# The feed-forward's first product as seven block products, its GELU moved behind the next copy, and sums moved to GpSimd and ScalarE

## The chip, the core and the metric

The kernel runs on one core of one Trainium2 chip. The time is device microseconds of one launch, from start to end. It was measured in three runs; their median is 1070.18 us, the lowest 1069.54 us, the highest 1071.64 us.

## What is computed

The input is a matrix of 4096 rows (tokens) of 256 numbers, all float32. Each row is normalised; the result feeds two branches, and the output is the input plus both.

```python
xn = layernorm(x)
# branch 1: attention in windows of 64 rows, then a feed-forward
x1 = xn + attention(xn) @ Wo + bo
x2 = layernorm(x1) * gamma + beta
h  = gelu(x2 @ W1 + b1)            # W1: 256 x 1024
branch1 = x2 + h @ W2 + b2         # W2: 1024 x 256
# branch 2: two of 8 experts for each token, weighted by their shares
branch2 = sum over the two of share * (silu(gate(xn) * up(xn)) @ down + bias)
out = x + branch1 + branch2
```

The change touches the last stage only: `h`, the second product, and the sum of everything.

## The kernel before, in words

Tokens are sorted by expert. A long first part of the kernel computes, in each step, attention for four of the eight heads of 256 tokens and one expert unit side by side; the experts' results are written to `done`, a table in device memory with one row for each (token, expert) pair. Some further units run under a condition. The last of them ends at 847 us on TensorE. From there on only the feed-forward is left.

The feed-forward works on eight groups of 512 tokens, `g = 0..7` (L1547 to L1576). The order of every engine's instructions is that of the code: nothing is rearranged, and each engine takes its instructions strictly one after another. In one turn of the loop, for group `g`:

- SyncE loads the rows of group `g + 2` (`second_loads`, L1186): `x2` (two buffers) and the input rows into the sum `acc` (four buffers).
- `hidden(g)` (L1222): the first product. The hidden units are eight blocks of 128; for each, two matmuls (one for each half of the 256 input features) of 128 x 512 run into one PSUM bank, and ScalarE takes the bank with bias and GELU into `hT`. There are seven banks for everything in this stage, used in turn.
- `second_base(g + 1)` (L1202): on VectorE, `acc += beta + b2`, `scaled = x2 * gamma`, `acc += scaled`, each over 1024 numbers a partition.
- `combined(g - 1)` (L1281): on VectorE, eight instructions add the rows of the two experts, times their shares, to `acc`.
- `turned2(g + 1)` (L1209): TensorE transposes `x2`, and ScalarE writes it with `gamma` and `beta` as `x2T`, the input of `hidden(g + 1)`.
- `second_norm(g + 2)` (L1190): ScalarE normalises the loaded rows.
- `picked(g)` (L1266): GpSimd issues eight gathers from `done`, one for 128 tokens and one of their two experts.
- `second(g - 1)` (L1289), the second product, of the group before: seven block products of 16 matmuls each, in place of eight (p1, p2, p6, p5, p7, p3, p4, in the order of the code), with sums of blocks prepared before and sums of results after. VectorE adds the results to `acc`. `sums_of_hidden(g)` (L1254) prepares this for the group's own second product: four additions of 1024 numbers a partition on VectorE, put between the pieces of `second(g - 1)`.
- SyncE stores `acc` of group `g - 1`.

At `g = 0` there is no second product and no transpose, so `hidden(0)` and `hidden(1)` follow one another on TensorE. The sums of W2's blocks are made once on GpSimd (`sums_of_weights`, L1248). On GpSimd there is nothing else in this stage but the gathers.

Of the kernel before, what the change touches and what calls it, by code (L numbers as in the profile page):

```python
# [32 lines left out]
F32 = mybir.dt.float32  # L33
# [3 lines left out]
ALU = mybir.AluOpType  # L37
# [66 lines left out]
def block_kernel(ctx: ExitStack, tc: tile.TileContext, a: dict, out: bass.AP):  # L104
# [1097 lines left out]
    def second_base(g, acc, x2):  # L1202

        scaled = accp.tile([P, TG, D], F32, tag="scaled", name=f"scaled{g}", bufs=1)
        nc.vector.tensor_tensor(acc, acc, bcast(beta_b2, TG, 1), ALU.add)
        nc.vector.tensor_tensor(scaled, x2, bcast(gamma, TG, 1), ALU.mult)
        nc.vector.tensor_tensor(acc, acc, scaled, ALU.add)

    def turned2(g, x2):  # L1209
        x2T = turns.tile([P, DC, G], F32, tag="x2T", name=f"x2T{g}")  # L1210
        for c in range(DC):
            pt = bank(f"pt2_{g}_{c}")
            for t in range(TG):
                nc.tensor.transpose(  # L1214
                    pt[:, t * P : (t + 1) * P], x2[:, t, c * P : (c + 1) * P], ident
                )
            nc.scalar.activation(
                x2T[:, c, :], pt, AF.Identity, bias=beta_c[:, c : c + 1], scale=gamma_c[:, c : c + 1]
            )
        return x2T  # L1220

    def hidden(g, x2T):  # L1222
        hT = hf.tile([P, FC1, G], F32, tag="hf", name=f"hf{g}")
        for f in range(FC1):
            ph = bank(f"ph{g}_{f}")
            for c in range(DC):
                nc.tensor.matmul(  # L1227
                    ph,
                    W1[:, c, f * P : (f + 1) * P],
                    x2T[:, c, :],  # L1230
                    start=(c == 0),
                    stop=(c == DC - 1),
                )
            nc.scalar.activation(hT[:, f, :], ph, AF.Gelu, bias=b1[:, f : f + 1])  # L1234
        return hT

# [28 lines left out]

    def picked(g):  # L1266

        ys = []
        for i in range(g * TG, (g + 1) * TG):
            for k in range(2):  # L1270
                y = got.tile([P, D], F32, tag="got", name=f"got{i}_{k}")
                nc.gpsimd.indirect_dma_start(  # L1272
                    out=y,
                    out_offset=None,
                    in_=done,
                    in_offset=bass.IndirectOffsetOnAxis(ap=slot[:, k, i : i + 1], axis=0),
                )
                ys.append(y)
        return ys

    def combined(g, acc, ys):  # L1281
        for n, y in enumerate(ys):
            t, k = n // 2, n % 2
            i = g * TG + t
            nc.vector.scalar_tensor_tensor(  # L1285
                acc[:, t, :], y, share[:, k, i : i + 1], acc[:, t, :], ALU.mult, ALU.add
            )

    def second(g, acc, hT, v):  # L1289

        t1, t2 = slice(0, 2), slice(2, 4)
        u = hf.tile([P, 2, P], F32, tag="u", name=f"u{g}")

        def product(n, left, right):
            pb = bank(f"s{g}_{n}").rearrange("p (t n) -> p t n", n=P)[:, 0:2]
            for t in range(2):
                for f in range(FH):
                    nc.tensor.matmul(  # L1298
                        pb[:, t, :],
                        left[:, f, t * P : (t + 1) * P],  # L1300
                        right[:, f, :],
                        start=(f == 0),
                        stop=(f == FH - 1),
                    )
# [12 lines left out]
        p6 = product(6, v[:, 1], V2[:, 1])  # L1317
        nc.vector.tensor_tensor(u, p6, u, ALU.add)
        add(t1, C2, u)
        yield  # L1320
        p5 = product(5, v[:, 0], V2[:, 0])
        add(t1, C2, p5)
        add(t2, C2, p5)
        yield
        p7 = product(7, v[:, 2], V2[:, 2])
        nc.vector.tensor_tensor(u, p7, u, ALU.add)
        add(t2, C1, u)
        add(t2, C2, u)
        yield
        p3 = product(3, v[:, 3], W2[:, F_HI, C2])  # L1330
        add(t1, C2, p3)
        yield
        p4 = product(4, hT[:, F_HI, B:], V2[:, 3])
        add(t2, C1, p4)
        yield
# [35 lines left out]
    for b in range(ALWAYS):  # L1371
# [63 lines left out]
        if b == STEPS:  # L1435
            att.close()
            wf = pool(ctx, "wf", right)
            accp = pool(ctx, "accp", right, bufs=4)
            V2 = wf.tile([P, 4, FC1 // 2, P], F32, tag="V2", name="V2")
            x2s = {n: second_rows(n) for n in range(2)}  # L1440
            W1, W2 = matrix(wf, "W1", F1, DC), matrix(wf, "W2", D, FC1)
            b1 = column("b1", FC1, wf)
            gamma, beta, b2 = (row(n, D, wf) for n in ("gamma", "beta", "b2"))
            gamma_c, beta_c = column("gamma_c", DC, wf), column("beta_c", DC, wf)
            beta_b2 = wf.tile([P, D], F32, tag="beta_b2", name="beta_b2")
            shift2 = wf.tile([P, NT], F32, tag="shift2", name="shift2")
            turns = pool(ctx, "turns", right, bufs=2)

            late = pool(late_done, "late", right)
            other.update({n: late for n in range(ALWAYS, BLOCKS, 3)})  # L1450
            load_unit(ALWAYS)
            for n in range(ALWAYS, BLOCKS):
                xs[n] = gather(n)
            x2s = {n: (second_inputs(n), x2) for n, x2 in x2s.items()}
        if b == STEPS + 1:
            sums_of_weights()
        if b == ALWAYS - 1:
            load_unit(ALWAYS + 1)
        if b + 1 < ALWAYS:
# [52 lines left out]


    x2Ts = {n: turned2(n, x2s[n][1]) for n in range(2)}

    for b in range(ALWAYS, BLOCKS):
        nc.gpsimd.memset(xs[b], 0.0)
# [18 lines left out]
    late_done.close()  # L1536
    experts_done.close()
    hf = pool(ctx, "hf", right, bufs=2)
    got = pool(ctx, "got", right, bufs=8)
    second_base(0, *x2s[0])  # L1540
    last = None

    def some(steps, n):
        for _ in range(n):
            next(steps, None)

    for g in range(NG):  # L1547
        if g + 2 < NG:
            x2s[g + 2] = second_loads(g + 2)
        hT = hidden(g, x2Ts.pop(g))  # L1550
        if g + 1 < NG:
            second_base(g + 1, *x2s[g + 1])
        if g > 0:
            acc = x2s.pop(g - 1)[0]
            combined(g - 1, acc, ys)
        if 0 < g < NG - 1:
            x2Ts[g + 1] = turned2(g + 1, x2s[g + 1][1])
        if g + 2 < NG:
            second_norm(g + 2, x2s[g + 2][1])
        ys = picked(g)  # L1560
        outs = second(g - 1, acc, *last) if g > 0 else iter(())
        some(outs, 2)
        sums = sums_of_hidden(g, hT)
        last = hT, next(sums)
        some(outs, 2)
        some(sums, 1)
        some(outs, 3)
        if g > 0:
            store(g - 1, 0, TG, acc)
    acc = x2s.pop(NG - 1)[0]  # L1570
    combined(NG - 1, acc, ys)
    outs = second(NG - 1, acc, *last)
    some(outs, 6)
    store(NG - 1, 0, 2, acc)
    some(outs, 1)
    store(NG - 1, 2, 2, acc)  # L1576
# [86 lines left out]
```

## Time and profile before

| | |
|---|---|
| median of three runs | 1070.18 us |
| the profiled execution: its own time | 1067.22 us |
| its span in the profile | 1065.5 us |
| DVE (VectorE) busy over the span | 755.9 us, 71% |
| ACT (ScalarE) busy | 572.0 us, 54% |
| POOL (GpSimd) busy | 586.8 us, 55% |
| from 901.3 to 928.5 us, one turn of the loop: PE, DVE, ACT, POOL busy | 27.20, 15.87, 9.05, 7.94 us |
| granted TensorE clock in that turn | 1.00 |

A profile row names an engine, a line of the code, the operation, what it writes and reads, how many instructions it stands for, and how long they took. PE is TensorE, DVE is VectorE, ACT is ScalarE and POOL is GpSimd. A matmul of float32 appears as two records. In a list in order of time, the first number is the start in us from the span's start, the second the duration, and a bracket at the end tells how long the engine had been idle and who released it. In a list of groups, the numbers after the bar are busy us and mean ns of one, then idle us before them with the releaser.

### The profile page before, as it was taken

What the parts mean: (1) busy time and instruction counts of PE and PEld (TensorE: products, weight loads), DVE (VectorE), ACT (ScalarE), POOL (GpSimd) and SP (SyncE); (2) the same over time, 40 slices, a digit from 0 to 9 for tenths busy, and PEclk for the clock granted to TensorE, in tenths of its full rate; (3) what the DMA queues carried; (4) which work ended last, traced back from release to release, by engine and by line L of the source; (5) the groups of instructions that cost most, each with busy time, mean ns of one, the idle gap of its engine ahead of it and who ended that gap; (6) DMA issues with size and microseconds to landing.
All of it is one profiled execution on the core that took longest, in us unless ns stands there. A gap on an engine that the chain in (4) does not pass through costs nothing. (4 is left out here: it accounts for less than half of the span.)

```text
span 1065.5 us, 20424 instructions
## 1 busy us (share of the span) xinstructions
PE 1056.0 (99%) x7278; PEld 859.9 (81%) x7278; DVE 755.9 (71%) x1852; ACT 572.0 (54%) x1329; POOL 586.8 (55%) x706
## 2 busy tenths in 40 slices
PE   9999999999999999999999999999999999999998
PEld 6578887887888888888888888888888757777778
DVE  6667876877787687788888988888542455555546
ACT  4527566656656557756665666566454353333320
POOL 5418765675666666776777777777520053222220
PEclk9999999999999999999999999999999999999999
DMA  8226444435345344534543544445585343333111
GB/s 282 81 91 217 140 158 164 165 139 184 120 155 187 111 156 164 193 139 166 173 168 130 189 163 165 139 173 179 179 272 179 134 136 109 100 99 98 61 60 41
DMA packets 61047, 158.67 MB, mean 149 GB/s; under 512 B 6576, under 2 KB 46896, under 8 KB 56208
## 3 DMA queue, kind: packets, MB, share of 16 engines
q1 hardware_dynamic: 53632, 139.33, 37.7%
q0 software_dynamic: 6480, 17.70, 5.2%
q8 instruction: 59, 0.97, 0.4%
q10 hardware_dynamic: 832, 0.30, 0.1%
q14 instruction: 44, 0.36, 0.1%
HBM read 135.43 MB, written 21.89 MB: 148 GB/s over the span
## 5 line engine op out<-in xcount | busy, mean ns | idle before, releaser
L839 PE MATMUL gu<-xsT,wg 128*128 128x256 f32 (+1 forms) x1632 | 362.8, 369 | 0.0
L839 PEld LDWEIGHTS gu<-xsT,wg 128*128 128x128 f32 x1632 | 288.8, 190 | 46.0 <-DVE nm L1057 9.0
L1272 POOL DMA_INDIRECT got<-done,slot x64 | 64.5, 1008 | 175.8 <-DVE acc L1285 106.9
L847 ACT ACTIVATE gs<-gu,wg 128x256 f32<-128x256 f32 (+1 forms) x204 | 92.0, 452 | 112.8 <-PE gu L839 108.4
L1084 POOL TENSOR_TENSOR pr<-pr 128x256 f32<-128x256 f32 x128 | 113.5, 887 | 64.1 <-ACT pr L1072 64.1
L848 DVE SCALAR_TENSOR_TENSOR hT<-gu,wg,gs 128x256 f32<-128x256 f32 (+1 forms) x204 | 91.9, 462 | 73.8 <-ACT gs L847 73.8
L1085 POOL TENSOR_TENSOR pr<-pr,ident 128x256 f32<-128x256 f32 x128 | 132.8, 1038 | 10.0
L1072 ACT ACTIVATE pr<-pr,nm 128x256 f32<-128x256 f32 x256 | 126.8, 497 | 1.0 <-ACT xsT L831 0.6
L1227 PE MATMUL ph<-x2T,W 128*128 128x512 f32 x256 | 111.0, 592 | 0.0
L1234 ACT ACTIVATE hf<-ph,b 128x512 f32<-128x512 f32 x64 | 43.8, 687 | 122.0 <-PE ph L1227 55.3
L880 ACT ACTIVATE hT<-hT 128x512 f32<-128x512 f32 (+2 forms) x179 | 84.9, 485 | 32.6 <-DVE hT L848 22.4
L1057 DVE CUSTOM_DVE_ANT_0 pr<-ps,mask 128x256 f32<-128x256 f32 x256 | 90.7, 420 | 16.1 <-PE ps L1043 16.1
L814 POOL DMA_INDIRECT xs<-xnd,token x71 | 68.8, 969 | 50.7 <-DVE paired_tiles L781 33.1
L1227 PEld LDWEIGHTS ph<-x2T,W 128*128 128x128 f32 x256 | 48.2, 190 | 57.9 <-issue 54.5
L1102 DVE TENSOR_TENSOR pr<-pr,rec 128x1024 f32<-128x1024 f32 x32 | 39.2, 1225 | 42.5 <-POOL pr L1084 42.5
L1115 POOL TENSOR_TENSOR xd<-xd,same 128x256 f32<-128x256 f32 x32 | 19.7, 615 | 84.2 <-DVE same L1113 84.1
L1308 DVE TENSOR_TENSOR acc<-u,acc 128x256 f32<-128x256 f32 x32 | 12.9, 423 | 68.4 <-ACT u L1311 67.9
L929 POOL TENSOR_TENSOR ts<-wd 128x384 f32<-128x384 f32 x54 | 54.0, 1000 | 2.1
L1072 ACT ACT_TABLE_LOAD x31 | 39.8, 1283 | 19.3 <-DVE nm L1057 19.3
L973 ACT COPY y<-sh 128x512 f32<-128x512 f32 x27 | 15.8, 586 | 62.3 <-PE sh L952 62.3
L1072 ACT ACTIVATION_READ_ACCUMULATOR pr<-pr,nm 128x1 f32 x256 | 48.3, 189 | 0.0
L952 PE MATMUL pe<-wd,hT 128*128 128x128 f32 x324 | 44.9, 275 | 0.0
(252 smaller groups left out, 2114.7 us busy)
## 6 DMA issues: line engine op xcount, KB each, us to landing
wg<-in_gate_up SPq DMA_DIRECT2D x37, 1670.5 KB, 7.1
wd<-in_down SPq DMA_DIRECT2D x37, 896.0 KB, 4.7
done<-y SPq DMA_DIRECT2D x30, 256.0 KB, 2.1
x<-in_x SPq DMA_DIRECT2D x8, 512.0 KB, 5.6
xnd<-xn SPq DMA_DIRECT2D x8, 512.0 KB, 4.9
res<-xnd SPq DMA_DIRECT2D x16, 256.0 KB, 2.9
x1d<-res SPq DMA_DIRECT2D x16, 256.0 KB, 2.2
x<-x1d SPq DMA_DIRECT2D x8, 512.0 KB, 4.7
```

What stands on the lines that cost most here:

```text
L814: nc.gpsimd.indirect_dma_start(out=x[:, t, :], out_offset=None, in_=xnd, in_offset=bass.IndirectOffsetOnAxis(ap=token[:, i : i + 1], axis=0),)
L839: nc.tensor.matmul(pb[:, k, :], w[:, lo : lo + P], xT[:, c, :], start=(c == 0), stop=(c == DC - 1),)
L847: nc.scalar.activation(gs, pb[:, 0, :], AF.Identity, bias=w[:, gb : gb + 1])
L848: nc.vector.scalar_tensor_tensor(hT[:, f, :], pb[:, 1, :], w[:, ub : ub + 1], gs, ALU.add, ALU.mult)
L880: nc.scalar.activation(hT[on, lo:hi, :], hT[on, lo:hi, :], AF.Silu)
L929: nc.gpsimd.tensor_tensor(out_, left_, right_, ALU.subtract)
L1057: nc.vector.tensor_tensor_reduce(out=pr[:, hh, j, :], in0=ps[hh][:, j, :], in1=mask[:, kinds[j], :], scale=-1.0, scalar=-LOWEST, op0=ALU.a ...
L1072: nc.scalar.activation(pr[:, hh, j, :], pr[:, hh, j, :], AF.Exp, bias=nm[:, j, hh : hh + 1], scale=-1.0, accum_out=sums[:, j, hh : hh + 1],)
L1084: nc.gpsimd.tensor_tensor(first, first, second, ALU.add)
L1085: nc.gpsimd.tensor_tensor(second, second, bcast(ident, 2, 1), ALU.mult)
L1227: nc.tensor.matmul(ph, W1[:, c, f * P : (f + 1) * P], x2T[:, c, :], start=(c == 0), stop=(c == DC - 1),)
L1272: nc.gpsimd.indirect_dma_start(out=y, out_offset=None, in_=done, in_offset=bass.IndirectOffsetOnAxis(ap=slot[:, k, i : i + 1], axis=0),)
```

## The change

The first product is done for pairs of hidden blocks, two blocks of 128 against the two halves of the features and the two halves of the tokens. Each of the four pairs takes seven matmuls of 128 x 256 in place of four of 128 x 512. The seven need sums of blocks of W1 (made once, `sums_of_first_weights`) and of `x2T` (for each group, `sums_of_inputs`), both on GpSimd. Their results are put together on ScalarE (one copy) and VectorE (five additions, each with one operand in PSUM) into `hT`, in SBUF. GELU then runs in place on `hT`: that of a pair is placed behind the next pair's copy on ScalarE, and that of the last pair behind the first copy of the second product.

`second_base` moves from VectorE to GpSimd, as twelve instructions of 256 numbers in place of three of 1024. The shares are multiplied into the gathered rows on ScalarE (`weighted`, eight instructions a group, between the copies and GELUs of the next group's `hidden`), and VectorE adds the rows with two instructions of 1024 numbers in place of eight of 256. The gathers of a group now go into one tile with two buffers, and stand ahead of `second_base` and `sums_of_inputs` on GpSimd. In the second product two pairs of additions become one instruction each.

```diff
     def second_base(g, acc, x2):
-        nc.vector.tensor_tensor(acc, acc, bcast(beta_b2, TG, 1), ALU.add)
-        nc.vector.tensor_tensor(scaled, x2, bcast(gamma, TG, 1), ALU.mult)
-        nc.vector.tensor_tensor(acc, acc, scaled, ALU.add)
+        for t in range(TG):
+            a_, s_ = acc[:, t, :], scaled[:, t, :]
+            nc.gpsimd.tensor_tensor(s_, x2[:, t, :], gamma, ALU.mult)
+            nc.gpsimd.tensor_tensor(a_, a_, beta_b2, ALU.add)
+            nc.gpsimd.tensor_tensor(a_, a_, s_, ALU.add)
...
+    def sums_of_inputs(g, x2T):
+        ts = turns.tile([P, 4, B], F32, tag="x2s", name=f"x2s{g}")
+        b11, b12, b21, b22 = x2T[:, 0, 0:B], x2T[:, 0, B:], x2T[:, 1, 0:B], x2T[:, 1, B:]
+        t1, t2, t3, t4 = (ts[:, k] for k in range(4))
+        for out_, left_, right_ in ((t1, b12, b11), (t2, b22, t1), (t3, b22, b12), (t4, b21, t2)):
+            nc.gpsimd.tensor_tensor(out_, left_, right_, ALU.subtract)
+        return x2T, ts
...
+        for m in range(FC1 // 2):
+            banks = [halves(bank(f"ph{g}_{m}_{k}")) for k in range(4)]
+            p1, p6, p7, p5, p2, p4, p3 = (banks[k // 2][:, k % 2, :] for k in range(7))
+            for to, left_, right_ in (
+                (p1, w[:, 0, 0, m, :], x2T[:, 0, 0:B]),
+                (p6, V1[:, 1, m, :], ts[:, 1]),
+                (p7, V1[:, 2, m, :], ts[:, 2]),
+                (p5, V1[:, 0, m, :], ts[:, 0]),
+                (p2, w[:, 0, 1, m, :], x2T[:, 1, 0:B]),
+                (p4, w[:, 1, 1, m, :], ts[:, 3]),
+                (p3, V1[:, 3, m, :], x2T[:, 1, B:]),
+            ):
+                nc.tensor.matmul(to, left_, right_, start=True, stop=True)
+
+            q = hf.tile([P, 3, B], F32, tag="q", name=f"q{g}_{m}", bufs=3)
+            both = hT[:, 2 * m : 2 * m + 2, :]
+            nc.scalar.copy(q[:, 0], p1)
+            nc.vector.tensor_tensor(q[:, 1], p6, q[:, 0], ALU.add)
+            nc.vector.tensor_tensor(q[:, 2], p7, q[:, 1], ALU.add)
+            nc.vector.tensor_tensor(both[:, :, B:], q[:, 1:3], bcast(p5, 2, 1), ALU.add)
+            nc.vector.tensor_tensor(both[:, :, 0:B], banks[2], q[:, 0::2], ALU.add)
+            nc.vector.tensor_tensor(both[:, 0, B:], p3, both[:, 0, B:], ALU.add)
+
+            if m > 0:
+                gelu(m - 1)
+            for _ in range(2 if m == 0 else 1):
+                next(others, None)
...
+    def weighted(g, ys):
+        for t in range(TG):
+            for k in range(2):
+                i = g * TG + t
+                nc.scalar.activation(
+                    ys[:, k, t, :], ys[:, k, t, :], AF.Copy, scale=share[:, k, i : i + 1]
+                )
+            yield
+
+    def combined(acc, ys):
+        for k in range(2):
+            nc.vector.tensor_tensor(acc, acc, ys[:, k], ALU.add)
...
     for g in range(NG):
         if g + 2 < NG:
             x2s[g + 2] = second_loads(g + 2)
-        hT = hidden(g, x2Ts.pop(g))
+        hT, ended = hidden(g, *x2Ts.pop(g), weighted(g - 1, ys) if g > 0 else iter(()))
+        ys_last = ys if g > 0 else None
+        ys = picked(g)
         if g + 1 < NG:
             second_base(g + 1, *x2s[g + 1])
+        if 0 < g < NG - 1:
+            x2Ts[g + 1] = sums_of_inputs(g + 1, turned2(g + 1, x2s[g + 1][1]))
+        acc = x2s.pop(g - 1)[0] if g > 0 else None
         if g > 0:
-            acc = x2s.pop(g - 1)[0]
-            combined(g - 1, acc, ys)
-        if 0 < g < NG - 1:
-            x2Ts[g + 1] = turned2(g + 1, x2s[g + 1][1])
+            combined(acc, ys_last)
+        outs = second(g - 1, acc, *last) if g > 0 else iter(())
+        some(outs, 1)
+        ended()
         if g + 2 < NG:
             second_norm(g + 2, x2s[g + 2][1])
-        ys = picked(g)
-        outs = second(g - 1, acc, *last) if g > 0 else iter(())
-        some(outs, 2)
+        some(outs, 1)
         sums = sums_of_hidden(g, hT)
```

More of the change, by code (lines that the diff above doesn't have):

```diff
@@ L1220, in turned2, with blocks_of_first @@
         return x2T
-    def hidden(g, x2T):
-        hT = hf.tile([P, FC1, G], F32, tag="hf", name=f"hf{g}")
[L1224 to L1235, printed above, removed]
+    def blocks_of_first():
+        return W1.rearrange("p c (m e q) -> p e c m q", e=2, q=P)
@@ new lines, in sums_of_first_weights @@
+    def sums_of_first_weights():
+        m = blocks_of_first()
+        a11, a12, a21, a22 = m[:, 0, 0], m[:, 0, 1], m[:, 1, 0], m[:, 1, 1]
+        s1, s2, s3, s4 = (V1[:, k] for k in range(4))
+        nc.gpsimd.tensor_tensor(s1, a21, a22, ALU.add)
+        for out_, left_, right_ in ((s2, s1, a11), (s3, a11, a21), (s4, a12, s2)):
+            nc.gpsimd.tensor_tensor(out_, left_, right_, ALU.subtract)
[4 more added lines that the diff above has]
+        for out_, left_, right_ in ((t1, b12, b11), (t2, b22, t1), (t3, b22, b12), (t4, b21, t2)):
+            nc.gpsimd.tensor_tensor(out_, left_, right_, ALU.subtract)
+        return x2T, ts
@@ new lines, in hidden, with gelu @@
+    def hidden(g, x2T, ts, others):
+        hT = hf.tile([P, FC1, G], F32, tag="hf", name=f"hf{g}")
+        w = blocks_of_first()
+        def gelu(m):
+            for f in range(2 * m, 2 * m + 2):
+                nc.scalar.activation(hT[:, f, :], hT[:, f, :], AF.Gelu, bias=b1[:, f : f + 1])
+        for m in range(FC1 // 2):
[23 more added lines that the diff above has]
+                next(others, None)
+        return hT, lambda: gelu(FC1 // 2 - 1)
@@ L1266, in picked @@
     def picked(g):
-        ys = []
-        for i in range(g * TG, (g + 1) * TG):
+        ys = got.tile([P, 2, TG, D], F32, tag="got", name=f"got{g}")
+        for t in range(TG):
+            i = g * TG + t
             for k in range(2):
-                y = got.tile([P, D], F32, tag="got", name=f"got{i}_{k}")
                 nc.gpsimd.indirect_dma_start(
-                    out=y,
+                    out=ys[:, k, t, :],
                     out_offset=None,
@@ L1277, in picked @@
                 )
-                ys.append(y)
         return ys
[L1281 to L1287, printed above, removed]
+    def weighted(g, ys):
+        for t in range(TG):
+            for k in range(2):
+                i = g * TG + t
+                nc.scalar.activation(
[5 more added lines that the diff above has]
+            nc.vector.tensor_tensor(acc, acc, ys[:, k], ALU.add)
     def second(g, acc, hT, v):
@@ L1321, in second @@
         p5 = product(5, v[:, 0], V2[:, 0])
-        add(t1, C2, p5)
-        add(t2, C2, p5)
+        right = acc.rearrange("p (k t) d -> p k t d", k=2)[:, :, :, C2]
+        nc.vector.tensor_tensor(right, right, bcast(p5, 2, 1), ALU.add)
         yield
@@ L1326, in second @@
         nc.vector.tensor_tensor(u, p7, u, ALU.add)
-        add(t2, C1, u)
-        add(t2, C2, u)
+        low = acc[:, t2, :].rearrange("p t (h n) -> p t h n", h=2)
+        nc.vector.tensor_tensor(low, low, bcast(u, 2, 2), ALU.add)
         yield
@@ L1439, in block_kernel @@
             V2 = wf.tile([P, 4, FC1 // 2, P], F32, tag="V2", name="V2")
+            V1 = wf.tile([P, 4, FC1 // 2, P], F32, tag="V1", name="V1")
             x2s = {n: second_rows(n) for n in range(2)}
@@ L1456, in block_kernel @@
             sums_of_weights()
+            sums_of_first_weights()
         if b == ALWAYS - 1:
@@ L1514, in block_kernel @@
     x2Ts = {n: turned2(n, x2s[n][1]) for n in range(2)}
+    x2Ts = {n: sums_of_inputs(n, x2T) for n, x2T in x2Ts.items()}
     for b in range(ALWAYS, BLOCKS):
@@ L1538, in block_kernel @@
     hf = pool(ctx, "hf", right, bufs=2)
-    got = pool(ctx, "got", right, bufs=8)
+    got = pool(ctx, "got", right, bufs=2)
     second_base(0, *x2s[0])
@@ L1570, in block_kernel @@
     acc = x2s.pop(NG - 1)[0]
-    combined(NG - 1, acc, ys)
+    list(weighted(NG - 1, ys))
     outs = second(NG - 1, acc, *last)
-    some(outs, 6)
+    some(outs, 2)
+    combined(acc, ys)
+    some(outs, 4)
     store(NG - 1, 0, 2, acc)
```

## The prediction

> **What bounds the kernel now.** I read the page's first rows, then the chain of waits that ended last, then the engines in order of time in the last stage, then a stretch where DVE and POOL work side by side.
>
> ```profile
> PE 1056.0 (99%) x7278; PEld 859.9 (81%) x7278; DVE 755.9 (71%) x1852; ACT 572.0 (54%) x1329; POOL 586.8 (55%) x706
> ```
>
> ```profile
> 846.76 27.47 PE ph L1227 x64
> 874.22 0.87 PE pt L1214 x8
> 875.10 12.51 PE s L1298 x112
> 887.60 13.73 PE ph L1227 x32
> 901.34 0.88 PE pt L1214 x8
> 902.21 12.51 PE s L1298 x112
> ```
>
> From 846.76 us the chain is PE alone, without a gap: `hidden(0)` and `hidden(1)` together, then for each group transposes, the second product of the group before, and the next first product. A turn takes 13.73 + 0.87 + 12.51 = 27.12 us. Only PE's work counts there, as long as nobody makes it wait.
>
> POOL, in the same stage, issues gathers only:
>
> ```profile
> 850.15 1.50 POOL L1272 DMA_INDIRECT got<-done,slot  x1 [56.10 <-DVE scaled L1206]
> 851.95 1.94 POOL L1272 DMA_INDIRECT got<-done,slot  x1 [0.30 <-issue]
> 854.20 0.95 POOL L1272 DMA_INDIRECT got<-done,slot  x1 [0.30 <-issue]
> 855.46 0.95 POOL L1272 DMA_INDIRECT got<-done,slot  x1 [0.30 <-issue]
> ```
>
> A gather costs 0.95 us and 0.30 us behind it: eight take 10.0 us. The first cannot start before 850.15, when the last expert rows are stored.
>
> What additions cost on POOL, and what they and DVE's do to each other, shows in the attention part:
>
> ```profile
> 511.35 0.93 POOL L1084 TENSOR_TENSOR pr<-pr 128x256 f32<-128x256 f32 x1 [1.00 <-ACT pr L1072]
> 512.35 0.93 POOL L1085 TENSOR_TENSOR pr<-pr,ident 128x256 f32<-128x256 f32 x1
> ...
> 515.06 0.72 POOL L1084 TENSOR_TENSOR pr<-pr 128x256 f32<-128x256 f32 x1
> ...
> 517.66 1.77 POOL L1085 TENSOR_TENSOR pr<-pr,ident 128x256 f32<-128x256 f32 x1
> ```
>
> ```profile
> 511.13 0.56 DVE L938 TENSOR_TENSOR ss<-hT 128x384 f32<-128x384 f32 x1
> 511.72 0.97 DVE L939 TENSOR_TENSOR ss<-ss,hT 128x384 f32<-128x384 f32 x1
> ...
> 514.40 0.69 DVE L1170 TENSOR_TENSOR res<-wo,res 128x512 f32<-128x512 f32 x1
> ...
> 517.62 1.23 DVE L1102 TENSOR_TENSOR pr<-pr,rec 128x1024 f32<-128x1024 f32 x1 [0.51 <-POOL pr L1084]
> ```
>
> A POOL addition of 128x256 takes 0.73 us alone. Beside a DVE instruction with two operands in SBUF it takes up to 1.77, and DVE's 0.56 becomes 0.97: they take turns. POOL ends 0.59 us after DVE's end (511.69 to 512.28), DVE's 384 numbers end 0.41 after POOL's (512.28 to 512.69). A DVE addition with one operand in PSUM (L1170) is not slowed and slows nobody.
>
> **PE: what is saved.** A record of 512 columns takes 13.74/32 = 0.429 us, one of 128 columns 12.51/112 = 0.112; on the line between them one of 256 takes 0.2176 (L839 at 810.72: 48 such in 10.45 us, the same). A group's first product becomes 4 pairs x 7 x 2 records x 0.2176 = 12.19 us, from 13.73: 1.54 less, 12.4 us for eight groups. A turn could be 25.57 us.
>
> **ACT: nothing.** A group needs 4 copies x 0.36 (L1311), 8 GELUs at 0.69 (L1234; from SBUF L880 shows 0.63), 8 `weighted` at some 0.5 (L1194, 0.59 with two scalars, the upper end; a copy, 0.36, the lower), and as before 1.4 + 2.1: some 14 of 25.6 us. A pair brings at most 0.36 + 1.3 + 2 x 0.5 = 2.7 us against PE's 3.05, so the next copy is not late. Built, it still has one table load in this stage.
>
> **DVE: fits alone.** Of a group's work `second_base` leaves (3 x 1.22), eight `combined` of 0.48 become two of 1.22, the second product loses two small instructions. The five additions of a pair take 2.6 us with the gaps between dependent ones (0.42 and 0.68 each), 10.4 a group, under PE's 12.2. All in all 10.4 + 2.4 + 4.7 (`sums_of_hidden`) + 4.3 = 21.8 us. Seven PSUM banks let it fall three banks behind.
>
> **POOL: fits alone, not beside DVE.** Sixteen additions of 128x256 come to the gathers. Rows near them: 0.61 (L1115, L1351, an operand repeated from one column), 0.73 (L1084 alone). These read two full operands, so 0.73; with the gaps 12 take 8.8 and 4 take 3.0. With 10.0 for gathers POOL's loop is 21.8 us, under 25.57. Before `hidden(g)` can run its second matmul, p6, POOL must have made t2.
>
> Here a rule of the Trainium skill speaks against the change. "SBUF — State Buffer", section "Who interferes with whom": a DVE instruction with two SBUF inputs contends with a GpSimd one that reads SBUF, and the one that comes first holds the port for its whole duration. By the rule, a DVE addition of 1024 and a POOL one of 256 in turn take 1.22 + 0.73 = 1.95 us. By the rows less, since the start of the waiting one (0.14 us) lies under the other: 1.07 (0.41 x 1024/384, less its start) + 0.59 = 1.66. I take the rows. Each wide DVE addition that meets POOL's then costs POOL 1.66 - 0.73 = 0.93 us.
>
> **The first two groups.** They have no second product between them, so PE leaves POOL little time.
> - PE: `hidden(0)` ends at 846.76 + 12.19 = 858.95.
> - POOL: gathers 850.15 to 860.15, then `second_base(1)`.
> - DVE: its last additions and the last GELUs (0.5 + 1.3) let `sums_of_hidden(0)` begin at 860.9; four wide ones in turn with POOL's last 6.6, to 867.5. POOL ends at 860.15 + 8.8 + 4 x 0.93 = 872.7.
> - `hidden(1)` fills its seven banks by 864.6, and waits for DVE to 868; with 0.7 more behind DVE it ends at 875.2. Transposes and `second(0)`: 888.6. p6 of `hidden(2)` is due at 889.0.
> - POOL: gathers 872.7 to 883.4 (0.7 of it behind `combined(0)`), `second_base(2)` 8.8 + 2.2 beside `sums_of_hidden(1)`, to 894.4; t1 and t2 to 895.9.
>
> So p6 waits 6.9 us. `hidden(2)` counts as begun at 895.9 - 0.44 = 895.5; before, 887.60: 7.9 us behind.
>
> **Then the loop.** With POOL last, its additions fall where DVE's two-SBUF ones do: gathers lie beside the first product (one operand in PSUM), additions beside `combined` and `sums_of_hidden`. Six wide ones cost 6 x 0.93 = 5.6, the additions of u (two of 256, one of 512) some 0.7. POOL's loop becomes 21.8 + 6.3 = 28.1 us, longer than PE's 25.57, so it stays last; and longer than the 27.12 of before. The next stall is PE at p6, 2.5 us in every turn. Five turns, to `hidden(7)`: 5 x 1.0 = 5.0. The last first product saves its 1.5; the end (last result, store) is unchanged.
>
> 7.9 + 5.0 - 1.5 = 11.4 us more. The profiled execution (1067.22, span 1065.5) would be 1078.6; it lies 3.0 below the median 1070.18, to which I add the sum: 1081.5.
>
> **Costed at nothing:** W1's sums (4 x 1.3 us), the first `sums_of_inputs` (8 x 0.73) and `second_base(0)` (8.8) on POOL. POOL is idle from 794 to 850 us, so they have 50 us of cover; without it they would add 20 us ahead of the first gather. The cleared rows behind them are needed at 822.7, they'd be ready at some 814. `picked(g)` now stands ahead of the additions: they wait for its 10 us, counted above. SyncE's load of `x2` for `g + 2` now waits for POOL's `second_base(g)`; the input rows' load and the store stand behind it. In the loop that addition is done before the turn begins and the rows are needed some 16 us into it, against 4.7 us to landing. The many waits for stored rows on DVE's third addition end by 849.7, 1 us late, which the banks cover.
>
> **Rivals.**
> - *POOL gets through* (faster). If POOL is hardly held up, the decisive point is t2 of group 2 and a loop under 25.57. Then: -12.4; `hidden(1)` still waits 2.3 for DVE's sums (to 865.6); POOL without delays has t2 at 860.15 + 8.8 + 10 + 8.8 + 1.5 = 889.2 against 887.3 due: 1.9. Sum -8.2: 1062. For it: POOL's free loop of 21.8 would gain 3.8 a turn. Against it: the 1.77 row.
> - *POOL's addition costs 0.62*, as the repeated-operand rows. The loop is 26.1, group 2 begins 5 late: 5 - 5 x 1.0 - 1.5: about 1069. Against it: 0.73 fits 0.46, 1.00, 1.27 for 128, 384, 512 numbers.
> - *The whole price of the rule.* A pair of 1.95 makes the loop 29.8: 5 x 2.7 in place of 5.0, and some 1 more at the start: 1091. The rows speak against it.
> - *PE not faster per column*: excluded by L839.
>
> **How the numbers follow.** Main case 0.55 (1081.5; 1074 to 1088 by 0.70 to 0.77 us for an addition), whole price 0.12 (1091), POOL cheap 0.13 (1069), POOL gets through 0.20 (1062). Slower: 0.55 + 0.12 + 0.02 of the third; same (0.2%, about what a measurement can tell from no change, 2.1 us) 0.06; faster 0.20 + 0.05. Range 1062 to 1090: it leaves out half of the first rival and of the whole price.
>
> **What would show it.** Right: p6 rows that wait for POOL from `hidden(2)` on, a turn of 28 us, POOL additions of 1.3 to 1.8 us beside DVE's wide ones and 0.73 beside the first product, DVE's wide ones up to 1.8; PE's 56 records in 12.2 us once p6 runs. Wrong: PE without gaps after 890 us, POOL waiting for ACT ahead of `sums_of_inputs`, a turn of 25.6 us. What would break the sum: POOL additions far from 0.73, or DVE, not POOL, releasing PE.

## The result, and the profile after

The changed kernel takes 1082.34 us (median of four runs, 1080.98 to 1082.86) against 1070.12 us for the kernel before on the same chip (1069.54 to 1071.64): 1.0111 times the time before, with a 95% interval of 1.0097 to 1.0125. The prediction was 1081.5 us, slower. The profiled execution of the changed kernel took 1082.58 us, with a span of 1080.8.

The first row of the page after: PE is busy for 97% of the span, before it was 99%, and POOL for 66% in place of 55%.

```profile
PE 1053.4 (97%) x7470; PEld 900.6 (83%) x7470; DVE 813.1 (75%) x1924; ACT 607.0 (56%) x1425; POOL 718.6 (66%) x838
```

The chain that ended last, in the last stage (start, length, what), shows who took over. Before, it was PE alone from 846.76 us. Now:

```profile
898.30 1.67 POOL x2s L1243
900.04 1.11 POOL x2s L1243 x2
...
902.61 0.99 POOL got L1319
...
929.11 1.23 POOL got L1319
...
1010.18 2.73 POOL x2s L1243 x2
1012.95 13.19 PE ph L1267 x52
1026.41 1.21 PE pt L1216 x8
1027.62 12.51 PE s L1349 x112
1040.13 12.09 PE ph L1267 x56
```

From the first gather at 852.36 to 1012.95 us, the last time that PE waits for it, the chain hardly leaves GpSimd: gathers, then `second_base`, then `sums_of_inputs`, then the next gathers. Only from there on does PE's own work set the end. PE's waits in the stage (us in total, times, longest) say the same from PE's side:

```profile
PE ph L1267 <- POOL x2s L1243: 8.4, 6, 2.9
PE ph L1267 <- DVE q L1272: 6.5, 1, 6.5
PE ph L1267 <- DVE hf L1274: 0.9, 2, 0.7
```

The taking of turns, seen at the place of the second row: first POOL's instructions, then DVE's of the same microseconds. Alone, POOL's take 0.73 us (866.50); the four that meet `sums_of_hidden(0)` take 1.59 to 1.71, and DVE's four 1.63 to 1.74 in place of 1.22 (the first three and two of them are shown; the last row is the same DVE addition before).

```profile
866.50 0.73 POOL L1207 TENSOR_TENSOR scaled<-x,gamma 128x256 f32<-128x256 f32 x1
867.19 1.71 POOL L1208 TENSOR_TENSOR acc<-acc,beta_b 128x256 f32<-128x256 f32 x1
868.98 1.59 POOL L1209 TENSOR_TENSOR acc<-acc,scaled 128x256 f32<-128x256 f32 x1
870.52 1.71 POOL L1207 TENSOR_TENSOR scaled<-x,gamma 128x256 f32<-128x256 f32 x1
```

```profile
866.58 1.73 DVE L1305 TENSOR_TENSOR hv<-hf 128x1024 f32<-128x1024 f32 x1 [1.40 <-ACT hf L1253]
868.34 1.63 DVE L1306 TENSOR_TENSOR hv<-hv,hf 128x1024 f32<-128x1024 f32 x1
```

```profile
861.25 1.23 DVE L1258 TENSOR_TENSOR hv<-hf 128x1024 f32<-128x1024 f32 x1 [6.92 <-ACT hf L1234]
```

Three stretches of the changed kernel by window (length, busy us of PE, PEld, DVE, ACT, POOL with their counts, granted clock, DMA share, GB/s) show what was not expected. After a wait PE doesn't go on at full speed: after the 6.47 us in `hidden(1)`, and after the 2.91 us in `hidden(2)`, the granted clock is low. In between it is 1.00.

```profile
873.70:884.00 10.30, 9.56 (x29) 7.49 (x30) 7.34 (x15) 6.12 (x12) 7.94 (x10) 0.66 0.55 175
884.00:893.00 9.00, 9.00 (x81) 8.90 (x81) 7.55 (x10) 4.90 (x9) 8.82 (x9) 1.00 0.11 31
901.00:904.60 3.60, 3.46 (x8) 2.78 (x9) 1.05 (x4) 1.97 (x5) 3.14 (x5) 0.53 0.63 185
```

### The profile page after: what moved, and what is told of

Read it like the earlier page. It is cut to its first block, busy times and chain, and to the rows that moved or that the text cites. A ratio compares the mean times of both kernels' runs of the same rounds, so it can differ in the third digit from the quotient of the medians.

```text
span 1080.8 us, 21176 instructions
## 1 busy us (share of the span) xinstructions
PE 1053.4 (97%) x7470; PEld 900.6 (83%) x7470; DVE 813.1 (75%) x1924; ACT 607.0 (56%) x1425; POOL 718.6 (66%) x838
## 5 line engine op out<-in xcount | busy, mean ns | idle before, releaser
L1271 ACT COPY q<-ph 128x256 f32<-128x256 f32 x32 | 11.8, 368 | 90.5 <-PE ph L1267 85.3
L1267 PE MATMUL ph<-x2s,V 128*128 128x256 f32 x192 | 50.6, 399 | 8.4 <-POOL x2s L1243 8.4
L1253 ACT ACTIVATE hf<-hf,b 128x512 f32<-128x512 f32 x64 | 42.7, 717 | 18.1 <-DVE hf L1276 15.7
L1267 PEld LDWEIGHTS ph<-x2s,V 128*128 128x128 f32 x192 | 37.7, 199 | 16.2 <-POOL x2s L1243 11.0
```

The source lines that it names most:

```text
L1267: nc.tensor.matmul(to, left_, right_, start=True, stop=True)
```

## The experiments

The theory is the prediction's: GpSimd's sixteen additions a group stand in one queue with the gathers, take turns with VectorE's additions of two SBUF operands, and t2, which p6 needs, comes last. The rivals are that VectorE takes over, that the order of GpSimd's queue alone decides, and, once it was seen, that TensorE's signals come late.

| kernel | edit to the changed kernel | us (before, same chip) | ratio, 95% interval |
|---|---|---|---|
| e1 | `second_base` back on VectorE | 1072.53 (1070.10) | 1.0019, 1.0011 to 1.0027 |
| e2 | gathers behind GpSimd's additions | 1080.94 (1070.10) | 1.0099, 1.0082 to 1.0116 |
| e3 | VectorE's six wide additions of a group with an operand in PSUM (leaves out part of the sums) | 1075.37 (1070.10) | 1.0047, 1.0030 to 1.0064 |
| e4 | e2, `sums_of_hidden(0)` behind `hidden(1)` | 1077.67 (1070.10) | 1.0073, 1.0056 to 1.0090 |
| e5 | e4, gathers of group 0 alone (leaves out seven groups' expert rows) | 1062.09 (1067.15) | 0.9952, 0.9937 to 0.9968 |
| e6 | e4, gathers beside the second product | 1058.19 (1067.15) | 0.9920, 0.9906 to 0.9933 |
| e7 | the kernel before, first product in halves | 1069.70 (1067.15) | one run |
| the changed kernel, second time | none | 1079.16 (1069.73) | 1.0089, 1.0072 to 1.0106 |
| e4, second time | | 1078.06 (1069.73) | 1.0081, 1.0064 to 1.0098 |
| e6, second time | | 1073.53 (1069.73) | 1.0035, 1.0022 to 1.0047 |
| the changed kernel, third time | none | 1080.63 (1070.62) | 1.0088, 1.0071 to 1.0105 |
| e5, second time | | 1061.72 (1067.34) | 0.9948, 0.9931 to 0.9964 |

Kernels that share a time of before ran on one chip. The chips turned out to be of two kinds (before at some 1070 and at some 1067 us), which is told below; a time is compared only with kernels of its own kind.

### e1: `second_base` back on VectorE

```diff
-        for t in range(TG):
-            a_, s_ = acc[:, t, :], scaled[:, t, :]
-            nc.gpsimd.tensor_tensor(s_, x2[:, t, :], gamma, ALU.mult)
-            nc.gpsimd.tensor_tensor(a_, a_, beta_b2, ALU.add)
-            nc.gpsimd.tensor_tensor(a_, a_, s_, ALU.add)
+        nc.vector.tensor_tensor(acc, acc, bcast(beta_b2, TG, 1), ALU.add)
+        nc.vector.tensor_tensor(scaled, x2, bcast(gamma, TG, 1), ALU.mult)
+        nc.vector.tensor_tensor(acc, acc, scaled, ALU.add)
```

> One part undone: the three wide additions of second_base are on VectorE again, all else as in the changed kernel. Theory (POOL comes last because its additions and VectorE's two-SBUF additions take turns): POOL's loop falls from 28 to some 13 us, so no p6 waits for POOL from group 2 on; VectorE's load rises to 21.8 + 3.7 = 25.5 us a turn, about PE's 25.57. Total 1062 to 1068 us. Rival (the loss is in the block product itself: its waits on copies and banks, or PE's slower clock without POOL as its cause): the turn stays near 28 us, total 1078 to 1083. Second rival (VectorE takes over as the bound): turns of 26.5 to 27.5 us, PE waiting for VectorE's bank releases, total 1068 to 1074.

1072.53 us, 9.8 below the changed kernel. Of PE's waits for POOL nothing is left:

```profile
PE ph L1265 <- issue: 5.8, 1, 5.8
PE ph L1265 <- DVE u L1375: 4.4, 5, 0.9
```

The first is `hidden(1)`'s wait, still there; the second is new, 0.87 us in each turn. In one turn (908.3 to 935.1 us) DVE is busy 25.77 of 26.80 us: once POOL is relieved, VectorE is the next bound, as the second rival has it, and the turn falls from a mean of 27.8 to 26.8 us only. So twelve additions on GpSimd cost the turn about 1 us against leaving them where they were, and VectorE could not have taken them and the five additions of a pair at PE's pace of 25.5.

### e2: gathers behind the additions

```diff
-        ys = picked(g)
         if g + 1 < NG:
             second_base(g + 1, *x2s[g + 1])
         if 0 < g < NG - 1:
             x2Ts[g + 1] = sums_of_inputs(g + 1, turned2(g + 1, x2s[g + 1][1]))
+        ys = picked(g)
```

> The same instructions on the same engines; only POOL's order in a turn is changed: second_base, sums_of_inputs, then the gathers, in place of gathers first. Theory (a matter of phase: POOL's additions meet VectorE's two-SBUF ones only because the gathers stand ahead of them): second_base(1) runs before the stage begins, the others run beside the first product, where VectorE's additions have an operand in PSUM; POOL additions show 0.73 there, no p6 waits for POOL, turns of 25.6 us, total 1060 to 1066 us. Rival (POOL's work is too much beside VectorE in any order): additions are still 1.6 to 1.7 us, the loop stays near 28 us, total 1078 to 1083. A middle result, turns near 28 us but the first 8 us saved, would give some 1074.

1080.94 us: 15 us or more above what was expected. On GpSimd things went as expected: no p6 waits for POOL, and `second_base` runs at 0.73 us beside the first product, from 899 us on. But turns take 26.5 us, not 25.6, as PE waits some 0.8 us in each for VectorE to empty a bank. The most is lost at the end: `hidden(7)` loses 10 us. Its PE rows, with the wait in brackets:

```profile
1035.45 0.59 PE L1267 MATMUL ph<-x2s,W 128*128 128x256 f32 x2
1038.49 0.70 PE L1267 MATMUL ph<-x2T,V 128*128 128x256 f32 x2 [2.44 <-issue]
1043.12 1.19 PE L1267 MATMUL ph<-x2T,W 128*128 128x256 f32 x2 [3.94 <-DVE hf L1274]
```

And the two that PE waited for, ScalarE and VectorE:

```profile
1037.60 0.37 ACT L1271 COPY q<-ph 128x256 f32<-128x256 f32 x1 [6.54 <-PE ph L1267]
```

```profile
1041.83 0.42 DVE L1273 TENSOR_TENSOR q<-ph,q 128x256 f32<-128x256 f32 x1 [3.40 <-remote]
```

The copy waits for PE, but the p6 it waits for had ended by 1030.5 us. PE waits for the copy, the copy for PE, and no work lies between them. The trace also holds the moments at which TensorE's signals (its semaphore's increments) arrived. Here they are beside the starts of the matmuls that send them; without delay one comes 0.3 us behind its start (the first two signals belong to senders ahead of the list):

```
senders   1028.16 1028.59 1029.02 1029.88 1030.75 1031.61 1032.04 1032.91 1034.80 1035.67 1038.81
signals   1029.00 1030.44 1031.86 1033.28 1033.32 1037.52 1041.81 1043.24 1043.29 1043.35 1043.40 1043.46 1043.51
gathers   sixteen, from 1019.79 on, most of them 1.25 us apart; the last begins at 1039.60
```

From 1029 us on the signals come 1.4 us apart, then 4.2 and 4.3, and six within 0.3 us, the first of them 1.2 us after the last gather had landed (1042.0).

### e3: an operand in PSUM for VectorE's wide additions

```diff
-        nc.vector.tensor_tensor(s1, a21, a22, ALU.add)
-        nc.vector.tensor_tensor(s2, s1, a11, ALU.subtract)
+        still = bcast(idle[0].rearrange("p a b n -> p (a b n)")[:, 0:B], FH, 1)
+        nc.vector.tensor_tensor(s1, a21, still, ALU.add)
+        nc.vector.tensor_tensor(s2, s1, still, ALU.subtract)
...
```

> Leaves out part of the work: the four additions of sums_of_hidden and the two of combined take as second operand a zeroed PSUM bank that is idle in this stage, in place of their second SBUF operand. Count, width and order of all instructions on every engine stay as in the changed kernel. Theory (two SBUF operands are what makes VectorE and POOL take turns): POOL's additions stay at 0.73 and VectorE's wide ones at 1.2, POOL's loop is 22 us, turns 25.6 us from group 3 on, total 1062 to 1067 us. Rival (POOL is late by its sheer number of instructions): POOL additions and turns as in the changed kernel, total 1079 to 1083.

1075.37 us, between what the theory and the rival gave. What the theory says of the queue holds: GpSimd releases PE not once. None of its additions in the loop takes over 1.5 us, and as long as nothing holds it up, its turn is 21.7 us; the prediction had 21.8 for a queue that takes no turns. The same groups of additions, first in the changed kernel, then here:

```profile
L1208 POOL TENSOR_TENSOR acc<-acc,beta_b 128x256 f32<-128x256 f32 x28 | 28.2, 1008 | 0.0
L1243 POOL TENSOR_TENSOR x2s<-x2T 128x256 f32<-128x256 f32 x12 | 15.8, 1318 | 0.0
```

```profile
L1208 POOL TENSOR_TENSOR acc<-acc,beta_b 128x256 f32<-128x256 f32 x27 | 20.2, 748 | 0.0
L1243 POOL TENSOR_TENSOR x2s<-x2T 128x256 f32<-128x256 f32 x12 | 8.9, 746 | 21.9 <-ACT x2T L1219 21.9
```

PE is still held up, in the main by `hidden(1)`'s wait, 3.1 in place of 6.5 us, and by gaps in the middle of its runs, 13 in all, put down to nothing visible:

```profile
PE ph L1267 <- DVE q L1272: 3.1, 1, 3.1
PE ph L1267 <- issue: 2.9, 7, 0.8
PE s L1352 <- issue: 2.5, 6, 0.8
```

So the taking of turns is what makes POOL last in the changed kernel. What is left after it fits the late signals, which this trace has too.

### e4: `sums_of_hidden(0)` behind `hidden(1)`

```diff
+        if g == 1:
+            sums = sums_of_hidden(0, last[0])
+            last = last[0], next(sums)
+            some(sums, 1)
...
+        if g == 0:
+            last = hT, None
+            continue
         sums = sums_of_hidden(g, hT)
```

> As the kernel with the gathers last, and the sums of the first group's hidden units stand behind the second group's first product on VectorE, not ahead of it. Theory (the wait inside hidden(1), 6.5 us and then a slow clock, is VectorE busy with these four wide additions): that wait goes, p6 of second(0) may wait up to 2 us for its sums instead; 3 to 5 us less than with the gathers last alone, 1056 to 1061 us. Rival (the wait comes from elsewhere, or moves whole to second(0)): the same as with the gathers last alone.

1077.67 us, 3.3 below e2. From the start of `hidden(0)` to the transposes behind `hidden(1)` it takes 29.28 us in place of 34.48: VectorE's four additions, on the way of the second group's banks, were the wait there. Part of the gain is given back later in the first turn; the end, 66.0 us from the last transposes against 54.4 in the changed kernel, stays.

### e5 and e6: gathers left out, gathers moved

Both edits are shown against e4.

```diff
-        ys = picked(g)
+        if g == 0:
+            ys = picked(g)
```

> Of the fourth kernel (GpSimd's sums ahead of its gathers, sums_of_hidden(0) late: 1077.7 us) only the gathers of group 0 are kept; every later group adds that group's rows again, so seven groups' expert rows are left out. In the fourth kernel's trace TensorE's signals that a matmul has ended come about 1.43 us apart while gathers land, and several at once when they have landed, so copies and additions are late though their matmul is long done. Theory A, the gathers hold up TensorE's signals: turns fall from 26.5 to 25.5-25.8 us, hidden(7) loses nothing (from its transposes to the end 54.4 us, as in the changed kernel, from 66.0), and the time is 846.6 + 29.3 + 5 x 25.6 + 54.4 + 1.6 = 1060 us (1058 to 1063). Rival B, the late signals come from the block product itself (six of them in 3 us) or from bank sharing: turns of 26.5 and the loss at hidden(7) stay, 1074 to 1078. Rival C, half and half: the loss at hidden(7) goes, since ACT no longer waits for rows that come late, but turns stay at 26.5: 1064 to 1067.

```diff
+        if g < NG - 1:
+            ys = picked(g)
         if 0 < g < NG - 1:
             x2Ts[g + 1] = sums_of_inputs(g + 1, turned2(g + 1, x2s[g + 1][1]))
-        ys = picked(g)
...
         ended()
+        if g == NG - 1:
+            held = hf.tile([P, 1], F32, tag="held", name="held", bufs=1)
+            end_ = hT[:, FC1 - 1, 0:1]
+            nc.gpsimd.tensor_tensor(held, end_, end_, ALU.add)
+            ys = picked(g)
```

> The fourth kernel with the gathers of a group put between second_base and sums_of_inputs on GpSimd, so that they lie beside the second product, where TensorE signals only every 1.79 us; those of the last group wait (by one small addition that reads hidden(7)'s last block) until hidden(7) is done. Nothing is left out. Theory A (gathers hold up TensorE's signals, which come closer than 1.43 us only in the first product): turns of 25.6 to 26.2 us (GpSimd's loop with 3 us of turns with VectorE is 25 to 26, so up to 0.6 of waiting for t2), end 54.5 to 56; total 846.6 + 28.5 + 5 x 25.9 + 55 + 1.6 = 1061 us (1058 to 1065), faster than before (1070.1). Rival B (late signals not from gathers): hidden(7) still loses about 10 us, turns 26.5: 1074 to 1078. Rival D (gathers beside combined's wide additions stretch to 1.5 to 1.9 us, and t2 comes last again): turns of 27 to 28, 1066 to 1072.

e5 took 1062.09 us and e6 1058.19, both faster than before (1067.15 on that chip). In both, turns are 25.47 us from the second on, and the end takes 54.3 us. e6, which computes everything, shows what the block product is worth when hardly anything holds it up, 9.0 us: PE's waits in the stage come to 2.9 us.

```profile
PE ph L1267 <- DVE u L1377: 2.1, 1, 2.1
PE ph L1267 <- DVE hf L1274: 0.6, 1, 0.6
```

The next kernel made it clear that this must not be read against e4, which ran on another chip.

### e7: the kernel before, in halves

```diff
-            ph = bank(f"ph{g}_{f}")
+            for h in range(2):
+                ph, part = bank(f"ph{g}_{f}_{h}")[:, :256], slice(h * 256, (h + 1) * 256)
...
```

> The kernel before, with each 128x512 block of the first product in two banks of 128x256 and two GELUs of 256 in place of one of 512; the same products, all computed. TensorE then signals every 0.86 us in the first product in place of 1.72. Theory A (while gathers land TensorE's signals come 1.43 us apart, whatever the kernel): beside gathers the GELUs of a first product begin some 1.5 us apart in place of 0.86, up to 4 us after their matmul's end, and several follow one another at once when the gathers end; TensorE waits a little for banks in hidden(g) where gathers fill more than half of it. Rival B (a trait of the block product's seven-product form): GELUs follow their matmuls by 0.3 us, 0.86 us apart, with gathers too. The time says little: 1070 to 1076 by A, 1069 to 1071 by B.

1069.70 us, and GELUs begin 0.86 us apart beside the gathers, none of them late. That looks like rival B. But the same trace has no late signal anywhere, nor have e5's and e6's, not even where the unchanged attention part gathers (759 to 770 us); there the changed kernel and e1 to e4 have six each, 0.7 to 2.4 us late. So it is not a trait of the kernels: the chip of e5 to e7 signals in time, and those of the kernels so far did not.

Counted over the last stage in all fourteen profiles (five of them are of runs told below). A signal is called late if it comes over 0.4 us behind its time, and "beside gathers" means 1 to 4.5 us after one was issued. In the first row 4 to 24 of some 210 signals in a profile have no record of their own, so its counts leave these out and pair the others with the senders that make them least late:

| | beside gathers | elsewhere |
|---|---|---|
| nine profiles on chips that signal late | at least 412 of 873 late | 0 of 905 late |
| five on chips that signal in time (before, e5 twice, e6, e7) | 0 of 301 late | 0 of 658 late |

The kernel before takes 1069.2 to 1071.8 us on the chips of the first kind and 1066.7 to 1068.6 on those of the second. Its only profile is from a chip of the second kind, so where it loses these 3 us is not known.

### Once more, side by side

> The changed kernel itself, beside the next two on one chip, since the kernels so far ran on two: in one (before 1070.1 us) TensorE's signals came late while gathers landed, in the other (before 1067.15 us) not once, not even where the unchanged attention part gathers. If this chip signals late: 1081 to 1083 us, as measured. If it signals in time: what stays is GpSimd's queue alone. Theory A (the prediction's: GpSimd's additions and VectorE's take turns, t2 comes last): waits of p6 for GpSimd from hidden(2) on, turns of 27 to 28.5 us, 1073 to 1079. Rival B (the late signals were most of it): turns of 25.5 to 26, 1060 to 1067.

> The fourth kernel (GpSimd's sums ahead of the gathers, sums_of_hidden(0) behind hidden(1)) again, all gathers kept. If this chip signals late: 1077 to 1080 us, with hidden(7) 10 us late. If in time: turns of 25.5 us and no loss at hidden(7), 1058 to 1062 us, which makes the late signals, not the sixteen gathers in a row, the cause of that loss. A time of 1074 or more with signals in time would say that the gathers hurt in another way.

> The sixth kernel (gathers beside the second product, those of the last group behind hidden(7)) again. If this chip signals in time: 1058 us as before, and no better than the fourth kernel beside it by more than 2 us. If it signals late: the second product's signals come 1.79 us apart, more than the 1.43 of the late ones, so little is lost: turns of 25.5 to 26 and 1060 to 1064 us, 14 or more below the fourth kernel.

This chip signals late. The changed kernel takes 1079.16 us and e4 1078.06, as on the others, and e4 is not told apart from the changed kernel. e6 takes 1073.53: 5.6 us below the changed kernel, but 3.8 above before, and 10 above what was expected of it. The same kernel has no late signal on e6's chip and at least 27 here. The expectation that the second product, with a signal every 1.79 us, would be spared is wrong. PE stops in the middle of it:

```profile
908.42 2.43 PE L1349 MATMUL s<-V,hv 128*128 128x128 f32 x18
911.17 0.27 PE L1349 MATMUL s<-V,hv 128*128 128x128 f32 x1 [0.32 <-issue]
911.92 0.59 PE L1349 MATMUL s<-V,hv 128*128 128x128 f32 x3 [0.47 <-issue]
913.34 4.69 PE L1349 MATMUL s<-V,hv 128*128 128x128 f32 x26 [0.84 <-issue]
```

Twelve such gaps take 5.1 us, and the turns are 25.5 to 29.6 us.

> The changed kernel once more, to have it on a chip that signals in time (before 1067.15 us there; the two where it ran so far signal late while gathers land). If this chip signals in time: by theory A (GpSimd's and VectorE's additions take turns and t2 comes last) the wait for VectorE in hidden(1) falls from 6.4 to 3 or 4 us and that for t2 of group 2 stays at 3 to 7, turns are 26 to 28 us, 1070 to 1078; by rival B (the late signals were most of it) turns of 25.5 and 1060 to 1066. If it signals late: 1079 to 1083 us again.

1080.63 us, on a chip that signals late again. The changed kernel has not been run on one that signals in time. In its three profiles PE waits for GpSimd 8.4, 5.7 and 9.9 us in the stage.

> The fifth kernel again (the fourth with the gathers of group 0 alone; seven groups' expert rows are left out), because it ran on the one chip that signals in time, while the fourth ran on two that signal late. If this chip signals late (before some 1070 us) and the gathers are the cause: late signals only up to 862 us, turns of 25.5 us from the second on, nothing lost at hidden(7) (54.4 us from its transposes to the end), 1062 to 1067 us against the 1077.7 and 1078.1 of the fourth. If such chips signal late for another reason that only falls together with the gathers: turns of 26.5 and 65 us at the end, 1075 or more. If this chip signals in time: 1062 us again, which settles nothing new.

1061.72 us, on a chip that signals in time: nothing new, as the expectation says. So a kernel without gathers in the loop has not been seen on a chip that signals late. The count above shows that late signals come with gathers. That they would go if the gathers went is not shown.

## Why the prediction was right

The prediction's sum was 11.4 us more. The medians, from one chip, lie 12.2 us apart; the spans of the profiled executions 15.3, since that of before is from a chip where it is 3 us faster. Which of the stretches hold these 3 us is not known. By stretches:

| | predicted | measured |
|---|---|---|
| to the start of `hidden(0)` | 0 | 848.93 - 846.59 = +2.3 |
| from there to p6 of `hidden(2)` (less 0.44) | +7.9 | 51.8 - 41.0 = +10.8 |
| from there to `hidden(7)`, five turns | +5.0 | 139.4 - 135.6 = +3.8 |
| the last first product and the end | -1.5 | 40.7 - 42.3 = -1.6 |

- **To the start.** The kernels ran to `hidden(0)` in 846.0 to 849.0 us, e2 and e3 with the same PE code in 846.7 and 846.6, so the changed code does not explain the 2.3 us. It is scatter from run to run, the kind of chip, or both. The profiled execution of before (1067.22) has no late signal and fits the chips of 1067; its median comes from one of 1070. Adding the 3.0 us was the right step, for a reason not known then.
- **PE's saving.** 1.54 us a group were predicted. `hidden(7)`, undisturbed, takes 12.09 us, and an undisturbed turn 25.47 (e6) against the 25.57 of the sum: right, and even a little more than predicted. (Eight times 1.54 is 12.3, not 12.4; nothing rests on it.) All of it was lost elsewhere.
- **Taking turns.** 1.66 us for a pair of a wide DVE and a POOL addition; the four pairs above take 6.65 us, 1.66 each. A whole price of 1.95 ("SBUF — State Buffer" in the Trainium skill, "Who interferes with whom", as quoted in the prediction) is not what the rows show: the waiting one's start lies under the other. That section says that the two contend, which agrees, and calls the ports that they share an exclusive lock; of the whole instruction it speaks for VectorE's two-port modes only.
- **The first two groups.** Predicted was a wait of 3.4 us in `hidden(1)` and one of 6.9 at p6; there were 6.47 + 0.74 and 2.91. `sums_of_hidden(0)` began at 866.58 in place of 860.9: 2.3 us from the start, and 2.6 in which VectorE waited for a p5 long done (p7 and p5 share a bank, and one signal): its signal came at 863.08, for a matmul begun at 859.51. Then the clock cost PE 3.1 us more. PE being late itself, the wait at p6 is shorter. What decides is t2, at 901.1 against 895.9: the gathers began 2.2 us late, and `second_base(2)` met more of VectorE's additions than counted. It took 13.65 us (884.61 to 898.26) where 11.0 were counted: five of its twelve are at 1.59 to 1.72 us in the trace, two at 0.91, and the first two of `sums_of_inputs`, counted at 0.73, at 1.70 and 1.05.
- **The loop.** 28.1 us predicted for GpSimd, with six additions a turn at 1.66 and 6.3 us lost by turns; from the gathers of group 2 (902.61) to those of group 6 (1013.74) it is 27.8, with five or six additions over 1.5 us in a turn and 4.9 to 6.5 us lost against 0.73 for each. But not every turn shows a wait of 2.5 us: PE waits for POOL 2.91, 0, 2.41, 0.23, 2.83 and 0 us in `hidden(2)` to `hidden(7)`. GpSimd's own turn varies from 26.5 to 28.8 us, and in `hidden(3)` and `hidden(7)` PE came later itself, with the slow clock behind the wait of the turn before. The mean holds, the single turn doesn't. The second and third run have a mean of 27.2 and 27.7; in the second, PE waits in `hidden(2)` and `hidden(6)` only, 3.23 and 2.45 us.
- **The rivals.** GpSimd didn't get through (8.4 us of waiting for it), its additions are 0.73 us and not 0.62, and the whole price of the rule was not paid. VectorE as the releaser, named as what would break the sum, came once, in `hidden(1)`, and not in the loop.
- **Nothing for the rest.** ACT keeps pace where signals are in time (e6), SyncE's loads and W1's sums are on no chain: right.

The clock was not in the sum at all. At the waits of 6.47, 2.91 and 2.83 us it stood at half for 10.24, 3.41 and 3.41 us, of which PE worked 6.2 + 3.4 + 3.4 us: 6.5 us lost. By the chain it changed the result little, because PE waited for GpSimd anyway. So did the late signals: between 852 and 1013 us none stands on the chain. They cost most in e2, e3, e4 and the second run of e6, where GpSimd no longer comes last. That the total fits to 0.8 us is in part luck: the start and t2 are 5 us later than predicted, of which up to 3 may lie in the kind of chip, and the loop is 1 us shorter.

What stays open: why some chips signal late while gathers land; whether there only the signal or the matmul's result itself is late, as the trace models the end of a matmul; and whether the changed kernel, with its queue on GpSimd, would be slower than before on a chip that signals in time. Its chain says so; no run does.

## What to carry to other kernels

Work moved to an idle engine is paid in that engine's queue: add up its loop with what it meets on the other side, and look at which of its results is needed first in the next turn. In e6 the same instructions and one small addition, in another order on GpSimd and with one group's sums later, take 1058 us on a chip that signals in time (before: 1067), and 1073.5 on one that signals late (before: 1069.7). And look at the chips before a comparison is believed: e4 against e6 looked like 19 us, on one chip it is 4.5.

## What the runs showed of the hardware

- On three of the five chips of the experiments TensorE's signals come late while gathers land, in e2's list up to 4.3 us apart, and then several at once. An engine that waits for TensorE then appears idle behind work that is long done, and TensorE itself stops between matmuls ("issue" gaps of up to 0.8 us in e3 and the second run of e6).
- TensorE's clock halves after short waits, but not after each. In the profiled execution it did at waits of 2.91 and 2.83 us (two, 2.40 and 0.43) and did not at 2.41 (1.98 and 0.43). In the second run 2.45 us was enough; in the third, 2.82 us (two waits) was so once, at 1039.6 us, and once not, at 983.8. The Trainium skill, "TensorE: Matmul & The Clock Gate", part 1, gives windows of about 3.4 us, the clock halved after an idle one. The slow stretches are 3.41 us or a multiple here, which agrees; but waits shorter than a window were enough. Where it happened, a wait of 2.9 us cost PE 1.7 us more.
- VectorE's additions of 128x1024 with both operands in SBUF and GpSimd's of 128x256 take turns, 1.66 us a pair; with one of VectorE's operands in PSUM, GpSimd's stay at 0.73 to 0.78 on average (e3).
- A gather is held up too. It takes GpSimd 0.95 us, but 1.94 beside VectorE's wide instructions with two SBUF operands (before, at 851.95 us) and 1.89 beside `sums_of_hidden` (e6, at 905.79). The prediction counted 0.95 for each, which fits the changed kernel, where most of them lie beside the first product (0.99 on average).
